# Per-head decay matrices from one row of exponentials per head, with the start of the kernel reordered, in a fused lightning-attention and router kernel

## The chip, the cores and the metric

The kernel runs on one core of a Trainium2 chip. The metric is device time in microseconds (us), from runs of the compiled program; beside it stands one profiled execution, whose trace gives the start and length of the instructions of each engine. The engines are TensorE (PE; its weight loads are shown apart as PEld), VectorE (DVE), ScalarE (ACT), GpSimd (POOL) and SyncE (SP, which issues most of the transfers; "SPq" is its queue). Each engine works through its own instructions in program order and waits on semaphores for the others.

## The reference, cut to what matters

The input is 4 x 512 tokens of 512 features; there are 16 heads of 128 and 64 experts.

```python
xn = layernorm(x)
qkv = silu(xn @ w_qkv.T)                       # per head: q, k, v of 128
# per head with slope s, over blocks of the sequence:
out = (q * exp(-s*pos)) @ kv + ((q @ k.T) * decay) @ v      # decay: exp(-s*(i-j)) for i >= j, else 0
kv  = exp(-s*block) * kv + (k * exp(-s*(block-pos))).T @ v
out = norm_w * out * rsqrt(mean(out*out) + eps)
s_  = (sigmoid(xn @ w_gate.T) * out) @ w_out.T
# router: softmax over 64 experts, the best 8 kept as weights
f   = xn * sum(topk_w) + topk_w @ expert_bias
y   = x + s_ * silu(f)
```

The kernel works in blocks of 128 tokens (P). Per head it needs a 128 x 128 matrix, exp(-s*(m-n)) for m >= n and 0 elsewhere, and 128 equal rows exp(-s*(m+1)).

## The kernel before, in words

Products in full precision are made of three passes of a rounded format: each operand is split into a high part (`split_hi`, L99, a cast on ACT) and a low part (`split_lo`, L102, a subtraction on the engine named), and a product is high by high, high by low and low by high. Large products go by a scheme of seven block products instead of eight: the list `PRODUCTS` (L39) names them A11*B11, S2*T2, S1*T1, A12*B21, S3*T3, S4*B22, A22*T4. The A and S come from weights (S are sums of the quarters of a weight, `sum_of`, L415), the B and T from the activations (T are sums of the quarters, `combine`, L278). Three PSUM banks carry a unit of seven; a later product with a fresh start writes over a bank that an earlier addition (`add`, L486, on DVE) has read.

**The v stage (up to about 190 us).** For 8 pairs of token tiles (two batches side by side; `tiles`, L874) the values v are made with a first set of weights `ws[0]`, then for all of them again with a second set `ws[1]`: 16 units in the loop of L928, k = 0 to 15. The first two units (`plain_unit`, L519) use the plain eight block products, since the sums aren't ready: A11*B11, A11*T1, A12*B21, A12*B22, then A21 and A22 likewise. Each result passes a sigmoid on ACT and a product on DVE (`silu_of`, L547; the product is put off by `deferred` until after the next block product), and is stored.

Each tile pair is prepared ahead of its unit (`prepare`, L816): "stats" (`layer_norms`, L223: mean and variance on DVE, the power -0.5 on POOL as `rstd`), "norms" (`normalise_x`, L240, two instructions on DVE), "turn" (eight transposes on PE, two copies from PSUM into `xf` on ACT), the splits and sums, and "logits" (16 small matmuls for the router and one addition on DVE).

The order on every engine is the order of the program text. Work for later tiles is hung into a unit through the lists `after[0]` to `after[6]`, one for each block product; in the plain units they are run in four groups (0; 1 and 2; 3 and 4; 5 and 6), after each quarter of the unit.

**The start (L879 to L926)** is written out by hand: loads of tile 0, of weights A11 and A12, of tile 1, of A21 and A22; 32 transposes of the identity to keep PE busy (`warm_up`, L143); the exponentials of the decays (`make_decays`, L166: one of 128 x 256 for each head on ACT), their masks (`mask_decays`, L171: a select on POOL for each head) and their 16 stores to memory, in three groups of 7, 5 and 4 heads; between them tile 0's preparation and the splits of A11, A12, A21 and A22. The decay tiles lie in the four buffers of the weight sums, so a sum can be written only after the store of what lay there.

**The heads (about 190 to 890 us).** For each head the weights are split, q, k and gates are made by units of seven, and attention for the head before is hung in between. `load_v` and `load_decay` (L649) bring a head's v and its decays from memory one head ahead; `scores_qk` (L660) uses the decays on DVE and POOL. The rest is the output product and the router's gate.

In the second half of the v stage the second weight set is split while PE works on units 6 to 8: the list at L956 gives, for each weight, the unit, the place in it, the engine, and which half. S4 in two halves on DVE stands at places 0 and 1 of unit 8 (n1 = 8).

## Time and profile before

| what | value |
|---|---|
| median of 3 runs | 1070.56 us (1069.88 to 1070.57) |
| the profiled execution | 1069.32 us, of which its span 1067.6 us |
| granted TensorE clock | 0.999 |
| busy: PE, PEld | 1055.7, 910.0 us |
| busy: DVE, ACT, POOL | 691.3, 482.3, 731.0 us |
| DMA, mean over the span | 134 GB/s, 143.09 MB |

The span runs from the first to the last instruction; the 1.7 us around it belong to the execution and not to any engine. Busy times of engines overlap. In the timelines, a line is: start in us, length in us (from the first to the last of a run of like instructions), engine, source line, operation, output and inputs by their names in the program, shapes, how many. What stands in brackets is the idle time of the engine just before it, and what released it. A "w_A_v" is a split weight, "blk_B" and "blk_T" split activations, "d_v" and "u_v" results of the plain units and the units of seven, "vo_v" what is stored of them.

### The profile page before, as it was taken

The numbers are of one execution on the slowest core, as the hardware profiler recorded it, in microseconds if no ns is written. First come the engines' busy times: TensorE is split into PE (matmuls) and PEld (weight loads), VectorE is DVE, ScalarE is ACT, GpSimd is POOL, SyncE is SP. The second block draws the span as 40 slices with busy tenths as digits, with TensorE's granted clock in tenths as the row PEclk, the third lists the DMA queues.
The fourth block names the chain that finished last, engine by engine and source line by source line (L and its number), as shares of the span: only waits on it lengthen the run. The fifth ranks groups of instructions, "written<-read, shape, count | busy, mean of one in ns | idle before, by whom it ended". The sixth has DMA issues, their size and how long they took to land.

```text
span 1067.6 us, 16505 instructions
## 1 busy us (share of the span) xinstructions
PE 1055.7 (99%) x5771; PEld 910.0 (85%) x5771; DVE 691.3 (65%) x1061; ACT 482.3 (45%) x938; POOL 731.0 (68%) x725
## 2 busy tenths in 40 slices
PE   9999999999999999999999999999999999999998
PEld 8788788888888888888888888888888887888886
DVE  5898776667576676655756656557566565754464
ACT  7545545544444444444444444444444444332221
POOL 6898793867788678777786787777867746612130
PEclk9999999999999999999999999999999999999999
DMA  8556745422422223234722242232222428364351
GB/s 273 194 181 241 268 153 178 140 92 85 139 84 94 83 94 111 95 124 171 278 85 66 84 128 85 85 125 88 85 75 88 135 80 285 94 189 173 88 197 50
DMA packets 105203, 143.09 MB, mean 134 GB/s; under 512 B 9120, under 2 KB 53536, under 8 KB 104224
## 3 DMA queue, kind: packets, MB, share of 16 engines
q1 hardware_dynamic: 104112, 141.33, 40.1%
q8 instruction: 46, 0.75, 0.3%
q10 hardware_dynamic: 1008, 0.70, 0.2%
q14 instruction: 37, 0.30, 0.1%
HBM read 91.14 MB, written 50.86 MB: 133 GB/s over the span
## 4 chain that ended last, share of the span: by engine, by line
PE 92%; DVE 3%; DMA 2%; ACT 1%; issue 1%; SPq 1%; POOL 0%; DVEq 0%; ACTq 0%; POOLq 0%
PE u_qk L496 28%; PE po L805 15%; PE u_g L496 14%; PE u_v L496 11%; PE o L702 5%; PE sa L665 5%; PE o L704 4%; PE ss L688 4%; PE kt L668 2%; DMA raw_v<-in_w_v_dram 1%; PE lg L314 1%; DVE vo_v L552 1%; PE pu L759 1%; DMA raw_eb<-in_expert_b_dram 1%; DVE sum_v L432 1%
## 5 line engine op out<-in xcount | busy, mean ns | idle before, releaser
L805 PE MATMUL po<-wr,yr 128*128 128x512 f32 (+1 forms) x777 | 179.7, 388 | 2.2 <-DVE u L798 1.0
L805 PEld LDWEIGHTS po<-wr,yr 128*128 128x128 f32 x777 | 144.2, 188 | 33.0 <-DVE u L798 1.2
L496 PE MATMUL u_qk<-blk_T,ws_qk 128*128 128x512 f32 x576 | 147.1, 395 | 0.0
L714 POOL TENSOR_TENSOR sqs<-sqs,sq 128x512 f32<-128x512 f32 x60 | 78.8, 1314 | 77.2 <-ACT sq L713 77.2
L496 PEld LDWEIGHTS u_qk<-blk_T,ws_qk 128*128 128x128 f32 x576 | 105.7, 188 | 20.4
L103 POOL TENSOR_TENSOR ws_qk<-sum_qk,ws_qk 128x512 fp32r<-128x512 f32 x64 | 82.9, 1297 | 30.4 <-ACT ws_qk L100 29.4
L103 DVE TENSOR_TENSOR yr<-yin,yr 128x512 fp32r<-128x512 f32 x64 | 69.1, 1095 | 47.0 <-ACT yr L100 47.0
L496 PE MATMUL u_qk<-blk_B,wa_qk 128*128 128x512 f32 x384 | 99.2, 393 | 0.0
L552 DVE TENSOR_TENSOR k<-k,sg_k 128x512 f32<-128x512 f32 x64 | 90.8, 1418 | 2.4 <-ACT sg_k L549 2.2
L702 PE MATMUL o<-at,vin 128*128 128x128 f32 x512 | 88.4, 275 | 0.0
L496 PEld LDWEIGHTS u_qk<-blk_B,wa_qk 128*128 128x128 f32 x384 | 70.9, 188 | 14.2
L692 DVE SCALAR_TENSOR_TENSOR st<-st,bdecay,ss 128x128 f32<-128x128 f32 x128 | 41.7, 346 | 60.7 <-ACT st L690 58.4
L549 ACT ACTIVATE sg_k<-k 128x512 f32<-128x512 f32 x64 | 40.5, 632 | 86.4 <-DVE k L487 86.4
L702 PEld LDWEIGHTS o<-at,vin 128*128 128x128 f32 x512 | 74.9, 191 | 2.5
L496 PE MATMUL u_g<-blk_T,ws_g 128*128 128x512 f32 x288 | 76.0, 400 | 0.0
L103 POOL TENSOR_TENSOR ws_g<-sum_g,ws_g 128x512 fp32r<-128x512 f32 x32 | 42.7, 1334 | 46.4 <-ACT ws_g L100 46.4
L704 PE MATMUL o<-qd,st 128*128 128x128 f32 x384 | 74.2, 275 | 0.0
L713 ACT ACTIVATE sq<-o 128x512 f32<-128x512 f32 x60 | 35.9, 598 | 72.3 <-POOL sqs L714 43.5
L767 POOL TENSOR_TENSOR u<-u,sgu 128x512 f32<-128x512 f32 x16 | 20.7, 1292 | 69.7 <-ACT sgu L766 60.4
L706 DVE SCALAR_TENSOR_TENSOR y<-o,nw,gt 128x512 f32<-128x512 f32 x64 | 47.6, 747 | 31.7 <-PE o L704 30.1
L665 PE MATMUL sa<-q,k 128*128 128x128 f32 x512 | 67.7, 275 | 0.2 <-DVE k L552 0.2
L665 PEld LDWEIGHTS sa<-q,k 128*128 128x128 f32 x512 | 64.3, 191 | 3.5 <-DVE q L552 0.7
(182 smaller groups left out, 2429.0 us busy)
## 6 DMA issues: line engine op xcount, KB each, us to landing
v<-vo_v SPq DMA_DIRECT2D x64, 256.0 KB, 2.0
raw_qk<-in_w_head_dram SPq DMA_DIRECT2D x64, 256.0 KB, 4.0
vin<-v SPq DMA_DIRECT2D x64, 256.0 KB, 3.6
y<-y SPq DMA_DIRECT2D x64, 256.0 KB, 2.1
yin<-y SPq DMA_DIRECT2D x64, 256.0 KB, 3.1
x<-in_x_dram SPq DMA_DIRECT2D x32, 256.0 KB, 4.6
raw_g<-in_w_head_dram SPq DMA_DIRECT2D x32, 256.0 KB, 3.1
raw_v<-in_w_v_dram SPq DMA_DIRECT2D x16, 256.0 KB, 5.3
```

The lines of the kernel that those rows point to most:

```text
L103: eng.tensor_tensor(lo, src, hi.bitcast(F32), ALU.subtract)
L496: nc.tensor.matmul(ps, lhsT, rhs, start=(first and c == 0 and n == 0), stop=(c == KC - 1 and n == len(PASSES) - 1), skip_group_check=not f ...
L549: nc.scalar.activation(sg, src, AF.Sigmoid)
L552: nc.vector.tensor_tensor(dst, src, sg, ALU.mult)
L665: nc.tensor.matmul(pa[:, c], k[:, c], q[:, c], start=True, stop=True)
L688: nc.tensor.matmul(ps[:, c], kd[s][:, c], v_of(b, h, c), start=True, stop=True)
L692: nc.vector.scalar_tensor_tensor(r[:, c], r[:, c - 1], bdecay[:, h : h + 1], ps[:, c], ALU.mult, ALU.add)
L702: nc.tensor.matmul(o, v_of(b, h, c), at[s][:, c], start=True, stop=(c == 0))
L704: nc.tensor.matmul(o, st[s][:, c - 1], qd[s][:, c - 1], start=False, stop=True)
L706: nc.vector.scalar_tensor_tensor(y, po, nw[:, h : h + 1], gts[s], ALU.mult, ALU.mult)
L714: nc.gpsimd.tensor_tensor(sq[b], sq[b], s1, ALU.add)
L805: nc.tensor.matmul(pos[t][:, c], yr[:, yi, bass.ts(t, P)], wos[h][:, wi, c], start=(h == 0 and n == 0), stop=(h in stops and n == len(PASS ...
```

## The change

It has four parts. (1) The decays: one tile of 16 rows (one per head) of 256 exponentials, in which the first 127 values are set to zero, takes the place of the sixteen tiles of 128 x 256. Its rows go to memory once; late in the v stage (units 13 to 15) each head's row is copied 128 times, from memory to memory. Since all 128 rows of such a copy are equal, reading it with a step of 255 instead of 256 shifts each row by one and gives the masked matrix: a head's load is now two transfers instead of one. (2) The start: a small sigmoid after the exponentials; tile 0's first half copied from PSUM by DVE, while ACT splits B11's high part from PSUM; B11's low part on POOL; the logits of tile 0 in two parts, one of them after unit 0's first quarter; A12's two halves swapped between DVE and POOL. (3) Norms of tile pair 1 ahead of the split of A21; stats of tile pair 2 ahead of the transposes of pair 1, and norms of pairs 2 and 3 at place 3 instead of 4. (4) S4's halves of the second weight set at places 1 and 2 of unit 8 instead of 0 and 1.

```diff
@@ -110,14 +110,18 @@
     ident = const.tile([P, P], F32, tag="ident", name="ident")
     ones = const.tile([P, 1], F32, tag="ones", name="ones")
     mhalf = const.tile([P, NT], F32, tag="mhalf", name="mhalf")
-    dist = const.tile([P, 2, P], F32, tag="dist", name="dist")
-    rest_of = const.tile([P, 1], F32, tag="rest_of", name="rest_of")
+    W = 2 * P
+    decay_row = const.tile([NH, W], F32, tag="decay_row", name="decay_row")
+    by_row = const.tile([P, 2], F32, tag="rest_of", name="rest_of")
+    rest_of, slope_of = by_row[:, 0:1], by_row[0:NH, 1:2]
     kdecay = const.tile([P, NH], F32, tag="kdecay", name="kdecay")
     bdecay = const.tile([P, NH], F32, tag="bdecay", name="bdecay")
 
 
 
-    decay_d = [dram.tile([P, 2, P], F32, tag=f"decay{h}", name=f"decay_{h}") for h in range(NH)]
+
+    rows_d = dram.tile([NH, W], F32, tag="decay_rows", name="decay_rows_d")
+    decay_d = [dram.tile([P, W], F32, tag=f"decay{h}", name=f"decay_{h}") for h in range(NH)]
     v_d = {
         (b, g): dram.tile([NT, P, VW], F32, tag=f"v{b}_{g}", name=f"v_{b}_{g}")
         for b in range(B) for g in range(NH // VH)
@@ -146,35 +150,29 @@
             nc.tensor.transpose(ps, ident, ident)
 
 
-
     def make_dist():
         nc.gpsimd.iota(
-            dist[:, 0, :], pattern=[[-1, P]], base=0, channel_multiplier=1,
-            allow_small_or_imprecise_dtypes=True,
-        )
-        nc.gpsimd.iota(
-            dist[:, 1, :], pattern=[[-1, P]], base=-1, channel_multiplier=0,
+            decay_row, pattern=[[-1, W]], base=P - 1, channel_multiplier=0,
             allow_small_or_imprecise_dtypes=True,
         )
         nc.gpsimd.iota(
             rest_of, pattern=[[0, 1]], base=1 - P, channel_multiplier=1,
             allow_small_or_imprecise_dtypes=True,
         )
-        nc.gpsimd.tensor_scalar(dist[:, 0, :], dist[:, 0, :], 0.0, None, ALU.min)
-
-
-    def make_decays(d, hs):
-        for h in hs:
-            nc.scalar.activation(d[h // 4][:, h % 4], dist, AF.Exp, scale=slopes[:, h : h + 1])
-
-    def mask_decays(d, hs):
-        for h in hs:
-            nc.gpsimd.affine_select(
-                d[h // 4][:, h % 4, 0], d[h // 4][:, h % 4, 0], pattern=[[1, P]],
-                compare_op=ALU.is_ge, fill=0.0, base=0, channel_multiplier=-1,
-            )
-        for h in hs:
-            nc.sync.dma_start(out=decay_d[h], in_=d[h // 4][:, h % 4])
+        nc.gpsimd.tensor_scalar(decay_row, decay_row, 0.0, None, ALU.min)
+
+
+    def make_decays():
+        nc.scalar.activation(decay_row, decay_row, AF.Exp, scale=slope_of)
+        nc.scalar.activation(kdecay, slopes, AF.Exp, scale=rest_of)
+        nc.scalar.activation(bdecay, slopes, AF.Exp, scale=-float(P))
+        nc.gpsimd.memset(decay_row[:, 0 : P - 1], 0.0)
+
+    def keep_rows():
+        nc.sync.dma_start(out=rows_d, in_=decay_row)
+
+    def keep_decay(h):
+        nc.sync.dma_start(out=decay_d[h], in_=rows_d[h : h + 1].to_broadcast([P, W]))
 
 
     stats = [const.tile([P, NT, 2], F32, tag=f"stats{b}", name=f"stats{b}") for b in range(B)]
@@ -244,14 +242,16 @@
     xfs = {}
 
 
-    def transpose(stage, p, j, t):
+    def transpose(stage, p, j, t, copy=True):
         b = p * PB + j
         if j == 0:
             xfs[p, t] = stage.tile([P, PB, FC, P], F32, tag="xf", name=f"xf_{p}_{t}", bufs=2)
         pt = ps_sc.tile([P, FC, P], F32, tag="sc", name=f"pt_{b}_{t}")
         for c in range(FC):
             nc.tensor.transpose(pt[:, c, :], xts[b, t][:, bass.ts(c, P)], ident)
-        nc.scalar.copy(xfs[p, t][:, j], pt)
+        if copy:
+            nc.scalar.copy(xfs[p, t][:, j], pt)
+        return pt
 
     def halves(xf):
         return xf[:, 0, 0:KC], xf[:, 1, 0:KC], xf[:, 0, KC:], xf[:, 1, KC:]
@@ -305,15 +305,21 @@
             nc.sync.dma_start(out=blocks_d[n][:, t], in_=blocks[p, n].bitcast(F32)[:, t])
 
 
-    def logits(stage, p, t):
-        if t == 0:
+    lg = {}
+
+    def logits(stage, p, t, js=range(PB)):
+        if t == 0 and 0 in js:
             scores[p] = stage.tile([P, PB, NT, E], F32, tag="scores", name=f"scores_{p}", bufs=2)
-        ps = ps_sc.tile([P, PB, E], F32, tag="sc", name=f"lg_{p}_{t}")
-        for j in range(PB):
+        if 0 in js:
+            lg[p, t] = ps_sc.tile([P, PB, E], F32, tag="sc", name=f"lg_{p}_{t}")
+        ps = lg[p, t]
+        for j in js:
             for c in range(FC):
                 nc.tensor.matmul(
                     ps[:, j], xfs[p, t][:, j, c, :], rw[:, c, :], start=(c == 0), stop=(c == FC - 1)
                 )
+        if PB - 1 not in js:
+            return
         nc.vector.tensor_tensor(
             scores[p][:, :, t, :], ps, rb[:, None, :].to_broadcast([P, PB, E]), ALU.add
         )
@@ -648,7 +654,11 @@
 
     def load_decay(p, h, attp):
         dec[p, h] = attp.tile([P, 2, P], F32, tag="dec", name=f"dec_{p}_{h}", bufs=3)
-        nc.sync.dma_start(out=dec[p, h], in_=decay_d[h])
+        rows = decay_d[h].rearrange("n m -> (n m)")[P - 1 : P - 1 + P * (W - 1)]
+        nc.sync.dma_start(
+            out=dec[p, h][:, 0], in_=rows.rearrange("(n m) -> n m", m=W - 1)[:, 0:P]
+        )
+        nc.sync.dma_start(out=dec[p, h][:, 1], in_=decay_d[h][:, P:W])
 
 
     def chunks(a):
@@ -884,46 +894,44 @@
     make_first()
 
     nc.scalar.activation(kdecay[:, 0:NT], mhalf, AF.Exp)
+    nc.scalar.dma_start(out=slope_of, in_=slope.rearrange("o h -> h o"))
     nc.scalar.dma_start(out=slopes, in_=slope.to_broadcast([P, NH]))
     nc.scalar.dma_start(out=rw, in_=router_w)
     nc.scalar.dma_start(out=rb, in_=router_b.to_broadcast([P, E]))
     nc.scalar.dma_start(out=nw, in_=norm_w)
     make_dist()
+    sig = small.tile([P, NT], F32, tag="var", name="table")
     warm_up(WARM)
     for i, n in enumerate(XN):
         block(0, i, xa if i < NX else xb, i)
         blocks[1, n] = blocks[0, n]
     for n in ["A21"] + [n for n, _, _, _ in PRODUCTS]:
         ws[0].place(n)
-    nc.scalar.activation(kdecay, slopes, AF.Exp, scale=rest_of[:, 0:1])
-    nc.scalar.activation(bdecay, slopes, AF.Exp, scale=-float(P))
-    ds = [
-        sump.tile([P, KC * VW], F32, tag=f"sum{i}", name=f"mkdecay_{i}").rearrange(
-            "p (h a m) -> p h a m", a=2, m=P
-        ) for i in range(4)
-    ]
-    hs = range(0, 7), range(7, 12), range(12, NH)
-    make_decays(ds, hs[0])
+    make_decays()
+
+    nc.scalar.activation(sig, mhalf, AF.Sigmoid)
     prep[0]["stats"]()
     prep[0]["norms"]()
+
+    pt = [transpose(stage, 0, j, 0, False) for j in range(PB)]
+    nc.vector.tensor_copy(xfs[0, 0][:, 0], pt[0])
+    b11, b12, b21, b22 = halves(xfs[0, 0])
+    split_hi(blocks[0, "B11"][:, 0, 0], pt[0][:, 0:KC])
     ws[0].split_one("A11", nc.vector, hi=True)
-    prep[0]["turn"]()
+    split_lo(nc.gpsimd, blocks[0, "B11"][:, 0, 1], b11, blocks[0, "B11"][:, 0, 0])
+    nc.scalar.copy(xfs[0, 0][:, 1], pt[1])
+    nc.sync.dma_start(out=xf_d[0], in_=xfs[0, 0])
     load_pair(stage, *tiles[2])
-    mask_decays(ds, hs[0])
     warm_up(6)
-    prep[0]["sums"]()
-    ws[0].split_one("A12", nc.gpsimd, 0)
-    ws[0].split_one("A12", nc.vector, 1)
-    prep[0]["logits"]()
+    split_blocks(0, 0, nc.vector, (("T1", b12), ("B21", b21), ("B22", b22)))
+    ws[0].split_one("A12", nc.vector, 0)
+    ws[0].split_one("A12", nc.gpsimd, 1)
+    logits(stage, 0, 0, [0])
     prep[1]["stats"]()
+    prep[1]["norms"]()
     ws[0].split_one("A21", nc.vector)
-    make_decays(ds, hs[1])
-    prep[1]["norms"]()
     load_pair(stage, *tiles[3])
-    mask_decays(ds, hs[1])
     ws[0].split_one("A22", nc.gpsimd)
-    make_decays(ds, hs[2])
-    mask_decays(ds, hs[2])
 
     for k, (p, t) in enumerate(tiles + again):
         g, after = k // n1, nothing()
@@ -936,13 +944,18 @@
             after[0 if k else 1].append(prep[k + 1]["turn"])
             if 0 < k < n1 - 3:
                 after[0].append(lambda k=k: load_pair(stage, *tiles[k + 3]))
+            if k == 0:
+                after[1].insert(0, prep[2]["stats"])
             after[1].append(prep[k + 1]["sums"])
             if k + 2 < n1:
-                after[1].append(prep[k + 2]["stats"])
-                after[4].append(prep[k + 2]["norms"])
+                if k:
+                    after[1].append(prep[k + 2]["stats"])
+                after[4 if k > 1 else 3].append(prep[k + 2]["norms"])
             after[1].append(prep[k + 1]["plain"])
             after[4].append(prep[k + 1]["more"])
             after[4 if k else 6].append(prep[k + 1]["logits"])
+        if k == 0:
+            after[0].append(lambda: logits(stage, 0, 0, [1]))
         if k < NP_FIRST:
             for i in range(2 * k, 2 * k + 2):
                 after[2 + 2 * (i % 2)].append(lambda i=i: ws[0].sum_of(i, nc.vector))
@@ -957,7 +970,7 @@
             ("A11", n1 - 2, 6, nc.gpsimd, None), ("S2", n1 - 1, 0, nc.gpsimd, None),
             ("S1", n1 - 1, 1, nc.gpsimd, None), ("A12", n1 - 1, 2, nc.vector, 0),
             ("S3", n1 - 1, 3, nc.gpsimd, None), ("A12", n1 - 1, 4, nc.vector, 1),
-            ("S4", n1, 0, nc.vector, 0), ("S4", n1, 1, nc.vector, 1), ("A22", n1, 0, nc.gpsimd, None),
+            ("S4", n1, 1, nc.vector, 0), ("S4", n1, 2, nc.vector, 1), ("A22", n1, 0, nc.gpsimd, None),
         ):
             if k == unit_of:
                 after[step].append(lambda n=n, eng=eng, piece=piece: ws[1].split_one(n, eng, piece))
@@ -967,6 +980,13 @@
             sums, split_plain, split_sums = combine(stage, 0, k - n1 - 1, nc.gpsimd, "r")
             after[1] += [sums, split_plain]
             after[4].append(split_sums)
+        if k == NP_FIRST:
+            after[0].append(keep_rows)
+        if n1 + NT < k < n1 + 2 * NT:
+            for j in range(1, len(PRODUCTS)):
+                h = (k - n1 - NT - 1) * (len(PRODUCTS) - 1) + j - 1
+                if h < NH:
+                    after[j].append(lambda h=h: keep_decay(h))
         if k == n1 + NT + 1:
             after[1].append(scores_exp)
         if k == 2 * n1 - 2:
```

## The prediction

> **What bounds the kernel now.** I read the page first.
>
> ```profile
> span 1067.6 us, 16505 instructions
> PE 1055.7 (99%) x5771; PEld 910.0 (85%) x5771; DVE 691.3 (65%) x1061; ACT 482.3 (45%) x938; POOL 731.0 (68%) x725
> ```
>
> TensorE runs 99% of the span, so an edit to another engine can only pay where PE stands still. Next the view of stretches, cut at PE's milestones (busy time of each engine, us):
>
> ```profile
> 10.23:17.80 7.57, 7.54 (x40) 6.24 (x41) 6.55 (x17) 5.67 (x13) 4.25 (x6) 1.00 0.98 329
> 25.90:40.45 14.55, 13.80 (x74) 11.36 (x74) 12.18 (x21) 8.22 (x17) 11.14 (x11) 1.00 0.61 218
> 40.45:52.70 12.25, 11.84 (x63) 9.53 (x62) 9.82 (x18) 6.99 (x16) 12.17 (x15) 1.00 0.52 170
> 64.80:100.00 35.20, 35.20 (x192) 30.14 (x190) 32.99 (x53) 17.61 (x42) 32.65 (x36) 1.00 0.58 208
> 100.00:122.00 22.00, 20.74 (x91) 16.46 (x91) 18.66 (x24) 13.56 (x22) 19.34 (x16) 1.00 0.67 238
> ```
>
> The first number is the stretch, the second PE's busy time. PE is solid from 64.8 to 100, and the same view has it solid from 122 to 190 and from 200 to 840; it loses time before 52.7 and between 100 and 122. Matmul ends are modelled, so I size the gaps by the starts of the weight loads. Then PE's timeline:
>
> ```profile
> 10.24 2.00 PE L314 MATMUL lg<-rw,xf 128*128 128x64 f32 x16 [0.44 <-ACT xf L254]
> 27.39 1.59 PE L528 MATMUL d_v<-w_A_v,blk_T 128*128 128x512 f32 x6
> 29.73 1.08 PE L253 MATMUL pt<-ident,x 128*128 128x128 f32 x8 [0.75 <-DVE x L204]
> 43.00 0.63 PE L253 MATMUL pt<-ident,x 128*128 128x128 f32 x4 [0.24 <-DVE x L204]
> 45.18 1.66 PE L496 MATMUL u_v<-w_S_v,blk_T 128*128 128x512 f32 x6 [0.17 <-DVE vo_v L552]
> 119.32 1.66 PE L496 MATMUL u_v<-w_S_v,blk_T 128*128 128x512 f32 x6 [1.15 <-DVE a_v L487]
> ```
>
> From 10.23 on PE never waits longer than half a microsecond until 28.7. Then tile 2's transposes are held by their norms, and the later gaps are DVE's too. Why DVE is late stands in the timelines of ACT and DVE:
>
> ```profile
> 15.69 2.10 ACT L168 ACTIVATE mkdecay<-dist,slopes 128x256 f32<-128x256 f32 x5
> 18.64 1.70 ACT L168 ACTIVATE mkdecay<-dist,slopes 128x256 f32<-128x256 f32 x4
> 20.36 1.28 ACT L549 ACT_TABLE_LOAD   x1
> 22.29 0.69 DVE L552 TENSOR_TENSOR vo_v<-d_v,sg_v 128x512 f32<-128x512 f32 x1 [4.17 <-ACT sg_v L549]
> ```
>
> DVE stood idle 4.17 us for the first sigmoid, which sat behind nine exponentials and a table load, and then worked almost without pause from 22.29 to 45. That backlog is what PE meets at 29.7, 42, 43 and 45.
>
> [...] The trace has 1.28 us, and the next activation starts 0.01 us later; I use 1.28. [...] the trace's PSUM adds take 0.69 (L487). [...] POOL's A12 half beside DVE's takes 1.79 us against 1.30 elsewhere. [...]
>
> **The change, part by part.** Estimated new times come from the old durations, each engine in its order.
>
> *The decay row.* Sixteen exponentials (2.89+2.10+1.70 = 6.7 us of ACT), sixteen POOL selects (2.93+1.72+1.02 = 5.7 us) and sixteen SP stores (issue spans 5.5 and 5.4 us, 2 MB) leave the start, as does the reuse of the sum buffers by the decay tiles. Added: one 256-wide exp (0.49, L168's duration) and a POOL memset (0.1 to 0.2, by the start's memsets). The iota and clamp are twice as wide and on half as many rows: 0.3 to 0.5 and 0.5 to 1.1 us, hidden by POOL's 3.3 us wait after them. The one danger is `slope_of`: memset waits for exp, exp for this DMA, and POOL's first rstd stands behind the memset. `slopes`, issued at 0.93, landed in 4.1; `nw`, the slowest of that queue, in 6.4. I take 4.1, at no cost: exp at 5.1 to 5.6, memset to 5.7, against the rstd at 5.71. At 6.4 the rstd is 2.3 late.
>
> *Sigmoid's table early.* 1.28 plus 0.2 us on ACT from about 6.0 to 7.5, when ACT next has work only at 8.1. Without that cover it would delay B11's high half one for one.
>
> *First blocks.* Before: both xf copies (to 10.67), 16 logits (10.23 to 12.0), first product at 12.04. Now DVE copies tile 0's first half at 8.45 to 9.1 (0.54 to 0.69 us); ACT makes B11's high half from PSUM at 8.1, A11's at 8.56 (its data lands at 8.48) to 9.6; POOL B11's low half by 9.9; DVE A11's lows by 10.6. PE finishes its six warm-up transposes at 9.7, then 8 logits (0.9) and the first product at 10.6. PE's unbroken work so begins at 9.7, not 10.23: 0.5 us (0.2 to 0.8; a loss if slope is late). The other 8 logits move behind the first 12 matmuls, same PE time.
>
> *A12's halves.* DVE's half needs the high part (ACT to 12.1) and ends at 12.8, POOL's at 13.9; PE reads them at 14.3 and 15.4. It now finds them ready: the 24 matmuls took 5.73 there against 5.47 in steady state (the chain's 56.35), so 0.3.
>
> *Norms ahead of A21.* Tile pair 1 (counted from 0): stats 12.8 to 14.9, rstd to 15.5, norms 15.5 to 16.6, PE free for the transposes at 17.0. A21's low parts queue behind, 16.6 to 17.9; PE reads its first at 18.3. Behind them on DVE are scores and the first product (18.1 to 18.7; before 22.29). SP's load of tile 3 waits as before for the transposes, and no early store stands behind it but the first v store, which comes later.
>
> *Tile 2's stats and norms earlier.* Its x landed at 18.6 and stats run at 19 to 21. POOL's rstd (21.5) now stands ahead of tile 1's four low blocks, which end at about 25, PE asking for the first at 25.1 and the last at 29: covered, thinly. norms end at about 24.5, ahead of S1's split (1.33) on DVE; PE wants them at 27.9. So the 1.06 us gap goes (weight loads: 28.64 to 29.70). S1 and S2 follow at 26 and 30, wanted after 40.
>
> *The later gaps.* At 42.1, 43.0 and 45.2 weight loads show 0.3+0.4+0.5 us. DVE, freed of 4 us of idle time, has 3 us in hand by then: 1.2, with 1.06 above 2.3. What ends last next is PE itself.
>
> *S4 one step later.*
>
> ```profile
> 117.99 0.68 DVE L103 TENSOR_TENSOR w_S_v<-sum_v,w_S_v 128x512 fp32r<-128x512 f32 x1
> 118.59 0.68 DVE L487 TENSOR_TENSOR a_v<-u_v,s_v 128x512 f32<-128x512 f32 x1
> 119.19 1.15 DVE L103 TENSOR_TENSOR w_S_v<-sum_v,w_S_v 128x512 fp32r<-128x512 f32 x1
> 120.27 0.68 DVE L487 TENSOR_TENSOR e_v<-u_v,a_v 128x512 f32<-128x512 f32 x1
> ```
>
> S3's product overwrites the bank that a_v reads, S4's the bank that e_v reads: PE waits for both. With S4's halves behind a_v and e_v, a_v ends 0.6 sooner, S3 starts at 118.7, e_v ends at 120.5 instead of 120.95, and S4's second half (to 121.5) meets its matmul at 121.6. Six products from 112.5 should end at 120.67 and end at 122.55: 1.9 lost. I take back 0.7 (0 to 1.5): DVE's products before a_v, [...] stay.
>
> *Decays later.* One 16 KB store of the rows goes out behind the second weight set's loads, near 52. 16 DRAM-to-DRAM copies issue at about 155 to 190, 0.4 us each on SP, between v stores. This kind is not in the trace; nearest are 1.8 us (idle) to 6.2 (crowded) to landing for the old decay stores. Head weights issued at 173.5 are first cast at 183.07: 9.6 us of cover, some 6 beyond a normal landing. In the heads, a second load adds 32 issues of 0.5. A decay issued at 246.8 is used at 272.5; the shortest lead seen, 195.0 to 213.7, leaves 14 us after a 4.2 us landing. Cost 0 (0 to 0.5); no gain, as PE is solid there.
>
> Sum: 0.5+0.3+2.3+0.7 = 3.8, less 0.2 for stalls left between steps: 3.6 us. The profiled execution took 1069.32 (span 1067.6 plus 1.7 around it), so 1065.7; the median 1070.56 lies 1.24 above it, so 1067.0.
>
> **The rivals.** *Main case*, gain 2.2 to 4.8: chance 0.76, most of it at 1066 to 1068.3; 5.1 is the ceiling, all gaps named plus 0.8 at the start. *DVE freed, but something else late*: POOL's tile 1 blocks behind the early rstd, or contention at the transition, eat the later gains; 0.5+1.06 stays, 1.6, time 1069.0, with 0 to 2.1 inside. For it: POOL is 11.1 of 14.55 us busy at 25.9 to 40.5. Against: 5.7 us of selects leave it. Chance 0.16. *Slope late*, the slower one: beyond a landing of 5.2 every microsecond moves the first rstd, the transposes and all behind. Against a gain of 3.6 it decides from a landing at 8.8 on, and passes +0.2% from 10.9; a landing at 11.5 gives 1073.3. For it: 4-byte pieces, one per partition, not in the trace. Against: `slopes` with 64-byte pieces took 4.1. Chance 0.08 with other slips, such as the head loads. *The change not doing what it says* would be DMA setting the start: the weights land at 8.5, 10.0, 14.7 and 16.1, all before my times, so it gets no share of its own.
>
> **How the numbers follow.** 0.2%, 2.1 us, is about what a measurement can tell from no change. Faster 0.76, same 0.16, slower 0.08. Range: 1065.3 (ceiling, with 0.2 for the runs' spread) to 1069.4 (gain 1.2).
>
> **What would show it.** Right: no L168 groups, table load near 6 us, first product near 10.6, sg_v near 17, the transposes at 29.7 and S1 at 45.18 some 2 and 3 us earlier with no gap, S3 behind a_v with under 0.6. Wrong: rstd after 6.3, PE gaps named POOL or DMA before 52, any gap at 190 to 215.

## The result and the profile after

| kernel | median | runs | ratio to before, 95% interval |
|---|---|---|---|
| before | 1070.01 us | 22 (1067.86 to 1072.05) | |
| changed | 1068.43 us | 22 (1065.74 to 1070.92) | 0.9982 [0.9977, 0.9988] |

The change saves about 1.9 us by the ratio (0.0018 of 1070.01), between 1.3 and 2.5; the two medians differ by 1.6. The predicted time was 1067.0, from a gain of 3.6. So the direction and the mechanism held, and the size came out at about half. One execution of a later kernel (s4_only) took 3454.54 us, three times the others, and is left out of its ratio. The profiled execution of the changed kernel took 1067.29 us (span 1065.5) against 1069.32 (1067.6): 2.0 us less.

From the page of the changed kernel, its span and the busy times:

```profile
span 1065.5 us, 16486 instructions
PE 1054.7 (99%) x5771; PEld 908.7 (85%) x5771; DVE 692.8 (65%) x1061; ACT 476.3 (45%) x923; POOL 727.2 (68%) x710
```

ACT has 15 instructions and 6.0 us less, POOL 15 and 3.8 us less, PE the same 5771 matmuls. Of the 2.1 us of span, 1.1 is idle time that PE no longer has (10.8 us now, 11.9 before) and 1.0 is busy time of the same matmuls, whose ends are modelled. The starts of the weight loads are therefore the better measure, and they are used below. Where time was won is seen in the stretches of the changed kernel (stretch, length, busy time of PE, PEld, DVE, ACT, POOL, then the granted clock and the DMA share):

```profile
9.80:16.80 7.00, 6.90 (x35) 5.27 (x33) 5.53 (x14) 4.51 (x8) 2.56 (x3) 1.00 0.89 310
25.50:40.30 14.80, 14.80 (x80) 12.55 (x79) 12.63 (x19) 7.59 (x15) 11.88 (x13) 1.00 0.42 144
40.30:50.00 9.70, 9.33 (x53) 7.80 (x52) 8.00 (x16) 5.87 (x13) 9.62 (x11) 1.00 0.57 193
98.00:120.00 22.00, 21.86 (x95) 17.33 (x95) 18.72 (x24) 13.66 (x21) 20.92 (x16) 1.00 0.73 263
180.00:190.00 10.00, 9.64 (x43) 7.67 (x42) 7.87 (x12) 6.04 (x12) 6.24 (x6) 1.00 0.69 224
```

PE is now whole from 25.5 to 40.3, and the transition (98 to 120) lost 0.14 us where the stretch from 100 to 122 lost 1.26 before. Still open is 0.37 us near 43. New is the loss in the last line: before, PE was solid there (10.00 of 10.00 from 180 to 190).

The timelines of PEld say what the weight loads wait for. Two lines of the kernel before, then those of the changed kernel:

```profile
45.18 1.23 PEld L496 LDWEIGHTS u_v<-w_S_v,blk_T 128*128 128x128 f32 x6 [0.59 <-DVE vo_v L552]
119.32 1.22 PEld L496 LDWEIGHTS u_v<-w_S_v,blk_T 128*128 128x128 f32 x6 [1.58 <-DVE a_v L487]
```

```profile
9.82 0.30 PEld L534 LDWEIGHTS d_v<-w_A_v,blk_B 128*128 128x128 f32 x2
10.47 0.79 PEld L534 LDWEIGHTS d_v<-w_A_v,blk_B 128*128 128x128 f32 x4 [0.34 <-DVE w_A_v L103]
16.82 0.88 PEld L251 LDWEIGHTS pt<-ident,x 128*128 128x128 f32 x8 [0.55 <-PE d_v L534]
27.59 1.02 PEld L251 LDWEIGHTS pt<-ident,x 128*128 128x128 f32 x8
42.88 1.22 PEld L502 LDWEIGHTS u_v<-w_S_v,blk_T 128*128 128x128 f32 x6 [0.81 <-DVE vo_v L558]
115.58 1.22 PEld L502 LDWEIGHTS u_v<-w_S_v,blk_T 128*128 128x128 f32 x6 [0.18 <-DVE a_v L493]
117.34 1.23 PEld L502 LDWEIGHTS u_v<-w_S_v,blk_B 128*128 128x128 f32 x6 [0.54 <-issue]
118.97 1.23 PEld L502 LDWEIGHTS u_v<-w_A_v,blk_T 128*128 128x128 f32 x6 [0.40 <-DVE vo_v L493]
182.19 1.23 PEld L502 LDWEIGHTS u_v<-w_A_v,blk_B 128*128 128x128 f32 x6 [0.78 <-ACT s_v L508]
```

The first product starts at 9.82 (12.04 before). Pair 2's transposes begin at 27.59 without a wait, and S1's product at 42.88 instead of 45.18, but still after 0.81 us of waiting for DVE. At the transition the wait for a_v has shrunk from 1.58 to 0.18, and a new one of 0.40 has come. At 182.19 there is a wait that the kernel before didn't have.

The timelines of ACT, DVE and POOL of the changed kernel show the cause that the prediction named, and the first sign of what it missed:

```profile
5.33 0.51 ACT L166 ACTIVATE decay_row<-decay_row,rest_of 16x256 f32<-16x256 f32 x1 [3.11 <-DMA x<-in_x_dram]
6.15 1.28 ACT L912 ACT_TABLE_LOAD   x1
17.07 1.29 DVE L103 TENSOR_TENSOR w_A_v<-raw_v,w_A_v 128x512 fp32r<-128x512 f32 x2
18.48 0.68 DVE L558 TENSOR_TENSOR vo_v<-d_v,sg_v 128x512 f32<-128x512 f32 x1
22.93 1.82 DVE L202 TENSOR_SCALAR x<-x,stats,rstd 128x512 f32<-128x512 f32 x2
24.67 2.36 DVE L103 TENSOR_TENSOR w_S_v<-sum_v,w_S_v 128x512 fp32r<-128x512 f32 x2
17.24 3.53 POOL L103 TENSOR_TENSOR w_A_v<-raw_v,w_A_v 128x512 fp32r<-128x512 f32 x2 [1.12 <-ACT w_A_v L100]
```

DVE's 4.17 us of waiting for the first sigmoid are gone: the product with it runs at 18.48 instead of 22.29. But A21's split on DVE (17.07) and A22's split on POOL (17.24) now begin within 0.2 us of each other, and POOL's takes 3.53 instead of 2.55.

**The measure used below.** All kernels have the same 5771 weight loads. The start of the i-th load of one trace, taken from the start of the i-th of the kernel before, gives the *lead* of that trace at that time, positive when it is ahead. Of the changed kernel it is 1.0 us at 18 us of the kernel before's time, 2.1 at 30 (the start of pair 2's transposes), 2.3 at 48 and at 117, 3.4 from 128 to 183, 2.8 from 187 to 980, and 2.2 behind that. So in this execution the full predicted gain was nearly there at 183 us; 0.66 were lost in unit 15, and 0.6 to a wait for the transposed router weights (`wTin`) at 980, a transfer that the change doesn't touch.

### The profile page after: what moved, and what is told of

It is laid out like the page before. It is cut to its first block, busy times and chain, and to the rows that moved or that the text cites. A ratio compares the mean times of both kernels' runs of the same rounds, so it can differ in the third digit from the quotient of the medians.

```text
span 1065.5 us, 16486 instructions
## 1 busy us (share of the span) xinstructions
PE 1054.7 (99%) x5771; PEld 908.7 (85%) x5771; DVE 692.8 (65%) x1061; ACT 476.3 (45%) x923; POOL 727.2 (68%) x710
## 3 DMA queue, kind: packets, MB, share of 16 engines
q1 hardware_dynamic: 108752, 141.35, 40.3%
## 4 chain that ended last, share of the span: by engine, by line
PE 84%; DMA 2%; DVE 2%; SPq 1%; issue 0%; ACT 0%; POOL 0%; DVEq 0%; ACTq 0%
PE u_qk L502 28%; PE u_g L502 14%; PE po L815 14%; PE o L712 5%; PE sa L675 5%; PE u_v L502 5%; PE o L714 4%; PE ss L698 4%; PE kt L678 2%; DMA yin<-y 1%; PE pu L769 1%; DMA v<-vo_v 1%; DMA wTin<-wTd 0%; DVE yr L103 0%; DVE u L808 0%; PE ssq L741 0%
```

## The experiments

The theories: the prediction's main case (DVE, freed from waiting for ACT, closes PE's gaps), against its rival that DVE is freed but something else is late. After the result two suspects for the missing part stood beside the main case: the copies of the decays hold something up in units 13 to 15, and A21's split meets A22's at 17 us. In the table "lead" is in us, at four times of the kernel before; "saved" is the median of the kernel before, run beside it on the same chip, less that of the kernel. Median and ratio are two estimates of one gain and lie up to 0.9 us apart (after_again: 1.1 by the medians, 2.0 by the ratio), so differences of under 1 us between two rows are not resolved.

| kernel | median | saved | ratio, 95% interval | lead at 30 | 48 | 128 | 210 |
|---|---|---|---|---|---|---|---|
| s4_only | 1069.15 | 0.8 | 0.9996 [0.9987, 1.0004] | 0.2 | 0.2 | 0.5 | 0.5 |
| decay_only | 1069.63 | 0.3 | 1.0000 [0.9992, 1.0008] | 0.1 | 0.9 | 0.8 | 0.3 |
| copies_in_heads | 1067.06 | 2.9 | 0.9979 [0.9969, 0.9989] | 2.3 | 2.1 | 3.3 | 3.3 |
| copies_twice | 1121.10 | -51.2 | 1.0487 [1.0472, 1.0501] | | | 3.5 | -48.8 |
| after_again | 1068.89 | 1.1 | 0.9981 [0.9970, 0.9992] | 1.8 | 1.9 | 3.0 | 3.0 |
| copies_spare | 1077.65 | -7.7 | 1.0072 [1.0059, 1.0085] | 0.0 | -0.2 | 0.9 | -8.9 |
| norms_as_before | 1068.48 | 1.5 | 0.9987 [0.9980, 0.9994] | -0.4 | 0.5 | 1.7 | 1.6 |
| heads_tail | 1065.70 | 4.3 | 0.9963 [0.9951, 0.9975] | 2.3 | 2.4 | 3.7 | 3.7 |
| a22_after | 1066.74 | 3.3 | 0.9973 [0.9964, 0.9982] | 1.4 | 1.7 | 2.8 | 2.8 |
| copies_units_9_to_11 | 1068.41 | 1.7 | 0.9982 [0.9974, 0.9990] | 0.1 | -0.1 | 1.0 | 1.0 |
| memset_late_best | 1065.04 | 5.0 | 0.9961 [0.9947, 0.9974] | -0.1 | 0.1 | 1.2 | 1.2 |
| a22_later | 1064.49 | 5.6 | 0.9950 [0.9937, 0.9963] | 2.2 | 2.4 | 3.5 | 3.5 |

**Part 4 alone (s4_only).** On the kernel before:

```diff
-("S4", n1, 0, nc.vector, 0), ("S4", n1, 1, nc.vector, 1),
+("S4", n1, 1, nc.vector, 0), ("S4", n1, 2, nc.vector, 1),
```

> The kernel before with part 4 alone (S4's halves at places 1 and 2 of unit 8). Theory, from the two traces: the waits of S3's and S4's products on a_v and e_v account for what was gained between 110 and 122 us. Then PE's lead over the kernel before is 0 until S3's product of unit 8 and 1.0 to 1.3 us after unit 8, and it stays to the end: time 1.0 to 1.3 us less. Rival: the 1.1 us at the transition came because DVE and POOL reached it less loaded after the new start; then part 4 alone gives the 0.6 us of one S4 half taken from ahead of a_v, or less.

The lead grows by 0.3 us at the transition, which is what the rival allowed, and the ratio can't be told from 1. The timeline of PEld of s4_only:

```profile
118.55 1.23 PEld L496 LDWEIGHTS u_v<-w_S_v,blk_T 128*128 128x128 f32 x6 [0.99 <-DVE a_v L487]
120.30 1.22 PEld L496 LDWEIGHTS u_v<-w_S_v,blk_B 128*128 128x128 f32 x6 [0.52 <-issue]
121.93 1.23 PEld L496 LDWEIGHTS u_v<-w_A_v,blk_T 128*128 128x128 f32 x6 [0.41 <-DVE vo_v L487]
```

a_v's wait goes from 1.58 to 0.99, as the step said (0.6 sooner), and 0.41 us of it come back two products later. DVE's timeline of the changed kernel shows why:

```profile
114.85 0.68 DVE L493 TENSOR_TENSOR a_v<-u_v,s_v 128x512 f32<-128x512 f32 x1
115.45 1.17 DVE L103 TENSOR_TENSOR w_S_v<-sum_v,w_S_v 128x512 fp32r<-128x512 f32 x1
116.55 0.68 DVE L493 TENSOR_TENSOR e_v<-u_v,a_v 128x512 f32<-128x512 f32 x1
117.15 1.17 DVE L103 TENSOR_TENSOR w_S_v<-sum_v,w_S_v 128x512 fp32r<-128x512 f32 x1
118.25 0.68 DVE L493 TENSOR_TENSOR vo_v<-u_v,e_v 128x512 f32<-128x512 f32 x1
```

S4's second half (117.15) now stands ahead of the addition into vo_v (118.25), which reads the bank that A22's product overwrites. The wait wasn't removed but moved, at a smaller price. In the whole change the transition brings 1.1 us (from 2.3 to 3.4), because there the wait for a_v falls to 0.18. What differs stands ahead of a_v on DVE, in the split of A12's second half (timelines of DVE, s4_only and the changed kernel):

```profile
111.03 1.75 DVE L103 TENSOR_TENSOR w_A_v<-raw_v,w_A_v 128x512 fp32r<-128x512 f32 x1
109.14 0.68 DVE L103 TENSOR_TENSOR w_A_v<-raw_v,w_A_v 128x512 fp32r<-128x512 f32 x1
```

It takes 1.75 us in the kernel before too (at 111.20), and 0.68 in decay_only. So part 4 alone is worth some 0.3 us of the 1.1; the rest came together with a split that took 0.68 instead of 1.75. The prediction didn't count on that, and no run shows what sets that length.

**Part 1 alone (decay_only).** The decays by one row and late copies, put on the kernel before; its start, norms and S4 are as before.

```diff
-    make_decays(ds, hs[0])
+    make_decays()
...
-    mask_decays(ds, hs[0])
...
+                    after[j].append(lambda h=h: keep_decay(h))
```

> The kernel before with part 1 alone (one row of exponentials per head, copies from memory to memory in units 13 to 15, two loads per head; the old order of the start, no early sigmoid, S4 as before). Theory: ACT's and POOL's freed time at the start removes part of PE's gaps before 45 us, 1 to 2 us, and the late copies bring the wait in unit 15 for the buffers of v, 0.4 to 1.0 us, shown as a DVE wait for the store of v near 180 us. Sum 0.2 to 1.5 us less. Rival: the wait in unit 15 of the changed kernel was a chance of that execution; then no such wait shows and the whole gain of the start is kept to the end.

Lead 0.9 us at 48, then 0.5 lost in unit 15 (PEld waits 0.66 there); the ratio is 1.0000. Pair 2's transposes no longer wait, though their norms stand in the old order; these end at 27.12, well before the 28.64 at which PE was free for them in the kernel before. So the exponentials were the cause of that gap. But the lead at 30 us is only 0.1, because A22's split, freed of the exponentials, now begins at 17.48 on POOL, and the second of pair 1's norms beside it takes 1.49 us instead of 0.55; between 16 and 20 us 1.3 us of lead go. The wait for a_v at the transition is still there as well, 1.77 us. Its profiled execution took 1072.53, the longest of its 13: its wait for the expert table was 1.2 us longer than before, its granted clock was 0.998 over the execution (0.999 before), and 0.59 went to `wTin` (lead -3.1 at the end).

**The copies moved to the heads (copies_in_heads).** On the changed kernel: two copies in units 9 and 10, the others one per head, two heads ahead of use.

```diff
-        if n1 + NT < k < n1 + 2 * NT:
...
+        if n1 < k <= n1 + 2:
+            after[2].append(lambda h=k - n1 - 1: keep_decay(h))
...
+        if p == 0 and kind == "qk" and n + 2 < NH:
+            after[2].append(lambda h=n + 2: keep_decay(h))
```

> The changed kernel with its 16 memory-to-memory copies taken out of units 13 to 15: heads 0 and 1 in units 9 and 10, the others one per head two heads ahead of use. Theory: the copies held v's stores in unit 15; no DVE wait for a store of v near 180 us is left and PE's lead at 200 us is the one it has at 122 us, about 0.66 us more than in the changed kernel, so the time is 0.5 to 0.8 us below it. Rival: the stores were held by the loads of the head weights that go out in unit 14; then the wait stays at 0.3 us or more.

The wait in unit 15 is gone, and the lead stays at 3.3. In the changed kernel it looks so (timelines of DVE and PEld):

```profile
180.25 0.69 DVE L493 TENSOR_TENSOR vo_v<-u_v,a_v 128x512 f32<-128x512 f32 x1 [2.53 <-DMA v<-vo_v]
182.19 1.23 PEld L502 LDWEIGHTS u_v<-w_A_v,blk_B 128*128 128x128 f32 x6 [0.78 <-ACT s_v L508]
```

DVE can't write the next vo_v before the store of an earlier one has landed, and all of PE's next results stand behind DVE. The trace of copies_in_heads has no wait of DVE for a store between 174 and 186. Of the lead 0.8 us is lost later, mostly to a wait of 1.1 for `wTin` at 933. In the times the edit can't be told from the change: 0.9979 against 0.9982.

**Each copy made twice (copies_twice), and once more with memory of its own (copies_spare).**

```diff
-                    after[j].append(lambda h=h: keep_decay(h))
+                    after[j] += [lambda h=h: keep_decay(h)] * 2
```

> The changed kernel with each of its 16 copies issued twice in the same place (the second writes the same values). Theory: SP and the transfer engines are then held twice as long between v's stores, so PE's wait in unit 15 grows from 0.66 us to 1.5 to 4 us and earlier units may show one too; time 1 to 3.5 us above the changed kernel. Rival (a chance of one execution, or the head weights' loads): the wait stays below 1 us.

This one measured something else. From the waits of SP's queue in copies_twice (us in total, times, the longest):

```profile
SPq L175 <- DMA decay<-decay_rows_d: 54.6, 16, 5.1
```

Writing the same memory again, each second copy waits for the landing of the first, and SP's queue with it: sixteen waits of 3.4 us on average. Together with what queued behind them (DVE waited 45.9 us for the stores of v between 150 and 260), that cost 52 us between 128 and 210; the granted clock over the execution was 0.979, against 0.999 in the changed kernel. It prices a queue that waits, not a copy.

```diff
         nc.sync.dma_start(out=decay_d[h], in_=rows_d[h : h + 1].to_broadcast([P, W]))
+        nc.sync.dma_start(out=spare_d[h], in_=rows_d[h : h + 1].to_broadcast([P, W]))
```

> The changed kernel with one more copy behind each of the 16, of the same row and size but into memory of its own that nobody reads, so that no copy waits for another one's landing (in the run with each copy issued twice into the same place SP waited 54.6 us for the first copy to land, so its 51 us more are not transfer time). Theory (the copies' transfer time and SP's issue time hold v's stores): PE's wait in units 14 and 15 grows from about 0.7 us to 2 to 6 us, time 1.5 to 5 us above the changed kernel. Rival (only SP's waits count, bandwidth is there): the wait stays under 1.2 us.

Without that wait, the timelines of DVE and PEld of copies_spare:

```profile
188.33 0.69 DVE L495 TENSOR_TENSOR vo_v<-u_v,a_v 128x512 f32<-128x512 f32 x1 [5.79 <-DMA v<-vo_v]
190.26 2.21 PEld L504 LDWEIGHTS u_v<-w_A_v,blk_B 128*128 128x128 f32 x6 [6.32 <-ACT s_v L510]
```

The same wait in the same place, 6.32 us instead of 0.78: doubling the copies makes it grow eightfold. Between 128 and 210 it loses 9.8 us, more than expected; behind the wait the six weight loads of the last line took 2.21 us instead of 1.23, and the granted clock over the execution was 0.995. From 0.78 to 6.32 us the cost grows faster than the number of copies. That it begins where the stores of v come back later than their buffer is wanted is the author's reading; two densities of copies don't prove it.

**The changed kernel once more (after_again).** No edit; a control, run on the same chip as the three kernels below it in the table.

> The changed kernel once more, as the control for the others of this group and as a second trace. If the wait in unit 15 belongs to the change, it is there again: DVE held by a store of v near 177 to 181 us and PE 0.4 to 1 us. If it was chance it is absent. The gain at 122 us should again be 3.0 to 3.6 us over the kernel before, and the rest of its loss, if any, should lie behind 885 us, in waits for transfers that differ from execution to execution.

Its 14 runs fall into two groups: six from 1065.99 to 1067.06 and eight from 1068.81 to 1071.38, with nothing between. The 22 runs of the same kernel in the result don't: they lie from 1065.74 to 1070.92 without a gap above 0.8 us, so the two groups may be chance. The profiled execution (1067.05) was of the first group. It again has DVE's wait for a store of v in unit 15 (1.9 us), but PE lost only 0.05 by it.

**Part 3 undone (norms_as_before).** Norms of pair 1 behind A21, stats of pair 2 and norms at place 4, as in the kernel before.

```diff
-    prep[1]["norms"]()
     ws[0].split_one("A21", nc.vector)
+    prep[1]["norms"]()
...
+                after[1].append(prep[k + 2]["stats"])
+                after[4].append(prep[k + 2]["norms"])
```

> The changed kernel with part 3 undone (tile pair 1's norms behind A21's split again; stats and norms of pairs 2 and 3 at their old places). Theory by the prediction's steps: the gap ahead of pair 1's transposes grows from 0.55 us to 1 to 1.8 us and a gap ahead of pair 2's transposes near 28 us of up to 1 us comes back, so PE's lead at 48 us falls from 2.3 to 1.0 to 1.6 us, time 0.7 to 1.3 us above the changed kernel. Rival (DVE and ACT freed by parts 1 and 2 are enough): the lead at 48 us stays at 2.0 or more.

In the trace waits are back ahead of pair 1's transposes (2.05 and 0.99 us), the lead at 48 us is 0.5, below what was expected, and from 128 on it is 1.7 instead of 3.4. In the medians part 3 is worth nothing: 1068.48 without it, 1068.43 and 1068.89 with it. So something takes back in the timed executions what it brings in the trace of the changed kernel. The timelines of DVE and POOL of norms_as_before show a candidate:

```profile
17.73 1.95 DVE L202 TENSOR_SCALAR x<-x,stats,rstd 128x512 f32<-128x512 f32 x2
17.95 2.87 POOL L103 TENSOR_TENSOR w_A_v<-raw_v,w_A_v 128x512 fp32r<-128x512 f32 x2 [1.77 <-ACT w_A_v L100]
```

A22's split on POOL comes just ahead of the second of pair 1's norms, which then takes 1.49 us instead of 0.54.

**A21 and A22.** With part 3 A21's split on DVE stands where the norms stood, and begins together with A22's on POOL. In copies_spare POOL came first (timelines of DVE, POOL and PEld):

```profile
17.43 3.46 DVE L103 TENSOR_TENSOR w_A_v<-raw_v,w_A_v 128x512 fp32r<-128x512 f32 x2
17.13 3.22 POOL L103 TENSOR_TENSOR w_A_v<-raw_v,w_A_v 128x512 fp32r<-128x512 f32 x2 [0.66 <-ACT w_A_v L100]
19.25 0.53 PEld L536 LDWEIGHTS d_v<-w_A_v,blk_B 128*128 128x128 f32 x3 [0.94 <-DVE w_A_v L103]
20.94 0.19 PEld L536 LDWEIGHTS d_v<-w_A_v,blk_B 128*128 128x128 f32 x1 [1.16 <-DVE w_A_v L103]
```

A21's split takes 3.46 us instead of 1.29, PE waits 2.1 us for it, and the lead at 30 us is 0.0 instead of 2.1. The start of POOL's instruction moves with the landing of its weight, that of DVE's with the norms, and in the traces either came first. With DVE ahead A21's takes 1.29 and POOL's up to 3.72 (2.55 in the kernel before); with POOL ahead, A21's takes 2.4 to 3.5, or the norms before it up to 2.9 instead of 1.0, and POOL's 2.7 to 3.2. So in these traces the one that came second lost the most; why they slow each other is not shown. With very close starts the records don't tell: in after_again POOL's begins at 17.39 and DVE's at 17.42, and it is POOL's that is longer (3.72). Of the eight traces that have the change's order here, DVE is undisturbed in five (lead at 30 us: 1.8 to 2.3) and slowed in three (copies_spare, copies_units_9_to_11, memset_late_best; lead -0.1 to 0.1).

So the collision was taken away, with all else as in the changed kernel:

```diff
     load_pair(stage, *tiles[3])
-    ws[0].split_one("A22", nc.gpsimd)
...
             if k == 0:
-                after[1].insert(0, prep[2]["stats"])
+                after[1].insert(0, lambda: ws[0].split_one("A22", nc.gpsimd))
+                after[1].insert(1, prep[2]["stats"])
```

> The changed kernel with the split of A22 (ACT's cast, then POOL's two subtractions) moved from ahead of unit 0 to behind its second quarter. In the changed kernel DVE's split of A21 and POOL's split of A22 start within 0.3 us of each other near 17 us; where DVE was first PE's lead at 30 us was 1.8 to 2.3 us, and in the one trace where POOL was first (copies_spare) DVE took 3.46 instead of 1.29 us and the lead was 0. Theory: this race, won by POOL in part of the executions, is a good part of what the median lost. Then the lead at 30 us is 1.5 to 2.3 us here, fewer executions lie 2 to 4 us above the fastest, and the median is 0.4 to 1.2 us below the changed kernel's (1068.4 and 1068.9). Rival: the spread comes from unit 15 and from behind 885 us alone; then the median stays within 0.3 us.

The timelines of DVE and POOL of a22_after:

```profile
17.74 1.28 DVE L103 TENSOR_TENSOR w_A_v<-raw_v,w_A_v 128x512 fp32r<-128x512 f32 x2
19.06 2.56 POOL L103 TENSOR_TENSOR w_A_v<-raw_v,w_A_v 128x512 fp32r<-128x512 f32 x2 [2.27 <-ACT w_A_v L100]
```

Both run at their undisturbed length, and eight of ten executions lie between 1065.82 and 1067.00. By the ratio it saves 2.9 us where the change saves 1.9 (by the medians 3.3 and 1.6), most of the predicted 3.6, with the copies still in units 13 to 15. The intervals of the two ratios (0.9964 to 0.9982 here, 0.9977 to 0.9988 for the change) overlap a little. The size fits: 2 us in three of eight traces is 0.8 us on average, an estimate. In this trace PE lost nothing in unit 15 (lead 2.8 throughout), so the trace doesn't rule out that part of the gain lies there. Its profiled execution took 1070.18 at a granted clock of 0.947 (the changed kernel's: 0.999); the leads behind 210 us are not read from it.

**The copies in units 9 to 11 (copies_units_9_to_11).**

```diff
-        if n1 + NT < k < n1 + 2 * NT:
+        if n1 < k < n1 + NT:
...
-                h = (k - n1 - NT - 1) * (len(PRODUCTS) - 1) + j - 1
+                h = (k - n1 - 1) * (len(PRODUCTS) - 1) + j - 1
```

> The changed kernel with its 16 copies in units 9 to 11 instead of 13 to 15, so that they are gone before the head weights load and before the reads of v. Theory (copies together with the head weights' loads hold v's stores; each alone does not): no PE wait in units 9 to 15, lead at 200 us equal to that at 128 us, time 0.5 to 1.5 us below the changed kernel, near copies_in_heads (1067.1). Rival (the copies alone hold v's stores wherever they stand): a PE wait of 0.3 us or more in units 9 to 11.

No wait in unit 15 (lead 1.0 from 128 to 210), and none for a store in units 9 to 11 either. The same 16 copies at the same density do no harm there. What differs in units 13 to 15 is that the loads of the first head's weights go out among them, and four stores of the router's scores (`scd`); that it is the weights is argued. In this trace POOL was ahead at 17 us, so the start's gain is missing. The median is that of the change; the 0.5 to 1.5 us that were expected below it did not come.

**The end, too (heads_tail), and both remedies (a22_later).** heads_tail is copies_in_heads with the transposed router weights of batches 1 to 3 loaded four steps earlier and batch 0's expert product one step later; a22_later adds the edit of a22_after.

```diff
-            m = h - (3 if b == 0 else 0)
-            if m == 0:
+            m = h - (4 if b == 0 else 0)
+            if b == 0 and m == 0:
                 load_wT(b, late)
+            if h == 12 and b + 1 < B:
+                load_wT(b + 1, late)
```

> The changed kernel with the copies spread over the heads, and in the output stage two waits on transfers taken away: the router's weights of batches 1 to 3 loaded four steps earlier, and batch 0's expert product one step later, so that the expert table has one step more to land. Theory: PE keeps the lead it has at 122 us (3.0 to 3.6) through unit 15, and gains 1 to 2.5 us more near 890 us and up to 0.7 for each later batch: 4.5 to 6.5 us below the kernel before, with a narrower spread. Rival (the waits move on to the next operand, the router's weights of batch 0 or the split of the table): under 1 us gained behind 885 us.

> The kernel of heads_tail with A22's split moved as in a22_after: copies in the heads, two waits on transfers taken away in the output stage, no race of A21 and A22. Theory: all three losses of the change are gone; 1064.5 to 1065.7 us with a spread under 2.5 us, 4.3 to 5.5 us below the kernel before. Rival (A22 late on POOL holds PE in unit 0's last quarter, its halves wanted from 20.8 us on): a new PE wait on A22 of 0.3 us or more near 21 us, and the time is that of heads_tail or above.

heads_tail saves 4.3 us (4.0 by the ratio; its interval lies clear of the change's), and its lead is 3.5 to 3.8 from 128 to the end, but for a dip to 1.9 near 895 us: no wait for `wTin` is left. The waits for the expert table (`ebs`: 0.57 and 1.17 us at 896 to 898 before) are gone too, but in these traces the lead doesn't rise there, for a reason told at the end. a22_later saves 5.6 us, ratio 0.9950 [0.9937, 0.9963], with five executions between 1064.29 and 1065.68, and no new wait near 21 us. It has the lowest median found, but its interval overlaps that of heads_tail. That the median lies 1.2 below heads_tail's, while the leads of the two traces agree (3.5 and 3.7), fits the collision, since in heads_tail's trace DVE was ahead; five executions of each don't show it.

**The memset later (memset_late_best).** The last rival from the prediction was a late slope: POOL's first rstd stands behind the memset, and that behind the exponential. Here the memset of heads_tail is moved to unit 2:

```diff
-        nc.gpsimd.memset(decay_row[:, 0 : P - 1], 0.0)
 
     def keep_rows():
+        nc.gpsimd.memset(decay_row[:, 0 : P - 1], 0.0)
```

> The kernel of heads_tail with POOL's memset of the exponentials' first 127 values moved from the start to unit 2, just ahead of the rows' store, so that POOL's first rstd no longer stands behind the chain slope transfer, exp, memset. In the traces of the changed kernel that rstd ran at 6.07 us while its operand was ready at 4.5. Theory (the rival of the prediction, at small size): rstd at 4.6, the first transposes 1.2 to 1.5 us sooner, but the weights A11 are cast at 8.8 to 9.3 as before, so the first products start at most 0.4 us sooner; time 0 to 0.5 us below heads_tail (1065.7). Rival (the slope chain sets the start): the first product 1.0 us or more sooner and the time 1 us less.

rstd begins at 4.71 instead of 5.91 in heads_tail, and the first product at 9.99 instead of 9.67: the start doesn't hang on the slope. The median is 0.7 below heads_tail's, within what five or six runs can tell. The six executions are 1063.87, 1064.56, 1064.94, 1065.14, then 1067.70 and, the profiled one, 1068.05. In that one POOL was ahead at 17 us (16.43 against 19.32).

## Why the prediction was right, and where its size was off

**The reading of the profile was right.** PE at 99% left only the stretches in which PE stands still, and at the start their cause was ACT's exponentials, by way of DVE. The first sigmoid's product moved from 22.29 to 18.48, the transposes' wait is gone, in decay_only too, and the lead at 128 us, 3.4 in the changed kernel and 3.0 to 3.7 in the other traces of its order with DVE ahead, meets the sum of 3.6. That it meets it so well is partly luck: the later gaps brought 0.2 instead of 1.2, and the transition 1.1 instead of 0.7. The start stood at about 0.8 in the sum (0.5 and 0.3); the lead at 18 us is 1.0. With the transposes, 1.9 was expected by 30 us, and it is 2.1. No L168 group of long exponentials is left, the table load is at 6.15, the first product at 9.82, ahead of the 10.6 expected.

**Part of the start's gain had another cause.** x landed 1.1 us sooner: its first statistics begin at 3.42 instead of 4.53. The traces with the new slope transfer, the first in ACT's queue, have them at 3.4 to 3.7, before and s4_only at 4.5. That this transfer is the cause is argued, not shown. The third matmul then waited 0.34 for A11's low half, so most of that microsecond was not used.

**The step that failed: "Norms ahead of A21".** The prediction placed A21's low parts at 16.6 to 17.9 and looked no further. It had seen POOL's A12 half take 1.79 us beside DVE's instead of 1.30, and at the start looked at no other such pair. In the kernel before, A22's split began at 18.82, behind its cast (17.70), which stood behind five exponentials on ACT, and behind POOL's selects; taking them away let it begin at 17.2, just when the moved norms had pushed A21 to 17.1. Two gains of the same change met. When POOL comes first, 2 us are lost, which is all of the start's gain. Undoing the move doesn't help: in norms_as_before and decay_only, with the earlier A22 beside them, it is the norms that take longer (the second 1.49 us in both, instead of 0.54 and 0.55). The term put at nothing was thus A22's split coming 1.6 us sooner, whatever DVE does then. The traces show this loss; how much of the missing 1.7 us in the median it makes up is inferred from a22_after, whose ratio is 1.0 us better.

**"Decays later", costed at 0 (0 to 0.5).** The prediction sized the cover of the head weights, which held, and asked nothing about the stores of v. Beside the copies these landed in 2.9 us (median) instead of 2.0, and DVE waits for them (2.53 us at 180.25). Of the five traces with the copies once in units 13 to 15 the lead lost 0.66 us in the changed kernel and 0.53 in decay_only, but 0.1 or less in after_again, norms_as_before and a22_after; with the copies elsewhere it lost nothing. The view of DMA issues, 150 to 190 us, gives the median landing of v's stores in the kernel before, then that of stores and copies in the changed kernel:

```profile
v<-vo_v SPq DMA_DIRECT2D x17, 256.0 KB, 2.0
```

```profile
v<-vo_v SPq DMA_DIRECT2D x17, 256.0 KB, 2.9
decay<-decay_rows_d SPq DMA_DIRECT2D x16, 128.0 KB, 4.4
```

The prediction expected 1.8 to 6.2 from the old stores. The copies' landing was sized; that v's stores would land later beside them was not. The doubled loads in the heads cost nothing (lead 2.8 at 210, 2.9 at 802), as said.

**"The later gaps", 1.2.** Only 0.2 came between 30 and 48. (The three waits are 0.33, 0.45 and 0.59 us in the view, 1.4 and not 1.2.) The first two, ahead of the transposes near 42, are gone. The third grew to 0.81. The prediction gave DVE 3 us in hand at 43, counted against the times of the kernel before; but PE, itself 2.5 us ahead by then, asks that much sooner. DVE had caught up, stood idle for 1.35 us at 29.6, and waited for POOL's rstd until 36.44. From there it had no pause (timeline of DVE of the changed kernel):

```profile
36.44 1.83 DVE L202 TENSOR_SCALAR x<-x,stats,rstd 128x512 f32<-128x512 f32 x2 [0.68 <-POOL rstd L236]
38.19 2.36 DVE L103 TENSOR_TENSOR w_S_v<-sum_v,w_S_v 128x512 fp32r<-128x512 f32 x2
42.15 1.27 DVE L558 TENSOR_TENSOR vo_v<-d_v,sg_v 128x512 f32<-128x512 f32 x2
```

The same run of work began at 39.27 in the kernel before, 2.8 us later, but S2's split took 1.84 there and takes 2.36 here; POOL is at work beside it in both. The product that S1 waits for thus came 2.3 us sooner (42.15 against 44.45), and PE 2.5. This is the part of the rival "something else late" that held.

**"S4 one step later", 0.7.** It is 0.3 alone, and the transition brings 1.1 in the change. The reason lies near the step's own sentence, that DVE's products before a_v "stay": how long the work ahead of a_v takes decides when it is ready, and A12's second half took 0.68 instead of 1.75. The new wait of 0.4 on vo_v was not named.

**What stays open.** How often POOL is ahead in untraced executions; how much of a run's spread is the wait in unit 15 and how much the waits for transfers behind 885 us, which differ from trace to trace. The kernel before spreads as much (1067.86 to 1072.05) without the collision, so the collision can't be the whole spread. The early sigmoid table was not tried by itself, nor the tail's edit without the others.

## What to carry to other kernels

When a change frees two engines, lay their next instructions side by side: a step that moves earlier can meet one that moves later, and then a few tenths of a microsecond decide over more than the step brings (here 0.3 us between two starts, and 2 us of lead). A cost of nothing for an added transfer must be asked of every transfer around it, above all of stores whose buffers are wanted again, and not only of the one it was scheduled beside. One trace shows one execution; look in several traces for an order that turns round.

## What was not expected of the hardware

- In six traces (heads_tail, a22_later and memset_late_best, and without the tail's edit a22_after, copies_spare and copies_units_9_to_11) the granted clock falls right behind three short waits of PE near 885 to 890 (near 900 in copies_spare): in heads_tail 0.69, 0.69 and 0.94 us, with one product between each. The stretches of heads_tail:

```profile
885.00:890.00 5.00, 4.99 (x15) 3.95 (x16) 2.28 (x3) 2.75 (x5) 2.95 (x3) 0.66 0.95 297
886.00:888.00 2.00, 2.00 (x6) 1.51 (x6) 0.69 (x1) 1.05 (x2) 0.69 (x1) 0.50 0.97 333
890.00:900.00 10.00, 10.00 (x50) 8.41 (x49) 5.00 (x7) 3.93 (x7) 7.53 (x6) 1.00 1.05 351
```

PE is busy all through the first stretch, with 15 matmuls in 5 us, where the last has 50 in 10. That costs some 1.6 us, an estimate from heads_tail's lead, which dips there from 3.5 to 1.9. In a22_after and copies_units_9_to_11 it hides itself: PE, later by about that much, waits for the expert table not at all and for 0.2 us (1.7 us before). A wait that is missing in one trace is thus no proof that it was removed. From 885 to 890 the granted clock is 0.66 in a22_later too; it is 0.77 there and 0.89 from 890 to 895 in memset_late_best and copies_units_9_to_11, 0.95 and 0.65 in a22_after (0.95 already from 16 to 30), and 0.87 and 0.79 in copies_spare (895 to 900, 900 to 905). In the kernel before, the changed kernel, after_again, norms_as_before, copies_in_heads, s4_only and decay_only it is 1.00 from 885 to 895, and PE has the three waits there as well: 0.68, 0.70 and 0.94 us in the kernel before. So the waits alone don't bring the fall, and what does is not shown.
- A copy of a 1 KB row 128 times from memory to memory (128 KB) landed in 4.4 us (median) beside other transfers; a second write to the same place held SP's queue until the first had landed (16 waits, 54.6 us, in copies_twice).
- The sigmoid's table load took 1.28 us and the activation after it began 0.01 us later (6.15 and 7.44), as in the kernel before.
